# Clearing a gather buffer on GpSimd ahead of every third batch, with a batch's last gather waiting for TensorE

## The chip, the core and the metric

The kernel runs on one core of a Trainium2 chip. The metric is the device time of one execution in microseconds (us). Each core has TensorE (PE; PEld is its weight load), VectorE (DVE), ScalarE (ACT), GpSimd (POOL) and SyncE (SP), each working through its own queue in order; they meet through semaphores. Matrix products land in PSUM, everything else on the chip lies in SBUF. GpSimd issues the indirect DMAs here: gathers that fetch rows of a table in HBM by an index for each partition.

## What is computed

One layer of a graph network with 12,500 nodes of 160 channels (64 scalars and 32 vectors of 3) and 400,000 edges. The edges are sorted by destination; sources are random. Cut to what matters:

```python
h  = relu(layernorm(x))                                  # 12500 x 160
s0, s1 = h0 @ W_sc0 * a, einsum(h1, W_sc1) * a           # own part of a node
y0, y1 = h0 @ W_l1_0 * a, einsum(h1, W_l1_1) * a         # what its edges carry
w  = silu(edge_length @ fc_W1 / 4) @ fc_W2 / 8           # 400000 x 192, weights of an edge
ys0, ys1 = y0[src], y1[src]                              # the gather
mid0 = concat(w_a * ys0 * e0,  w_d * dot(ys1, e1) / sqrt(3))
mid1 = concat(w_b * ys0 x e1,  w_c * e0 * ys1)
z0, z1 = scatter_add(mid0, dst), scatter_add(mid1, dst)  # sums by destination
out = x + C_S * s + C_X * concat(z0 @ W_l2_0, z1 @ W_l2_1) * a
```

## The kernel before

The first stage makes `y` for all nodes and writes it to `y_d` in HBM. The main stage, of which the change is a part, goes through the 400,000 edges in 3125 tiles of 128 edges, an edge on each partition. Four tiles (`GT`) make a batch; there are 782 batches (`NB`), the last but one with two tiles and the last with three.

For one batch `b` the work goes through the engines like this:

- `load(b)`, L571 to L584: GpSimd issues one gather per tile (L579), 128 rows of 160 floats out of `y_d`, into a slice of the batch's buffer `yg` of 128 x 4 x 160. `yg` has eleven buffers (`YB`). For 24 of the batches, named in `made_at`, no gather is made: TensorE computes the rows from gathered rows of `x`, in pieces spread over earlier batches.
- `hidden(s)`, L592, and `activate`, L597: the inner layer of the edge weights, for two batches at a time.
- `weigh(b)`, L609 and L611: TensorE makes the edge weights in one of two PSUM banks `pw`; ScalarE puts the edge's vector beside them.
- `lift_rows(b)`, L521: ScalarE multiplies each gathered slice by a scalar of the edge, into `yge`. It is the first to read `yg`.
- `dots_of(b)`, L526 and L528, and `products(b)`, L532 to L537: VectorE forms the messages `pr` from `pw`, `yg` and `yge`. L528 writes a part of `yg`. L537 is the last reader of the batch's `pw`.
- `select(u)`, L628: VectorE makes the one-hot matrices `sel` for three batches.
- `sums(b)`, L648: TensorE adds the messages by destination. At the end of a group of 24 or 12 tiles the sum is turned (L662), mapped (L675) and added to the result (L693).

The loop over batches writes these down in an order by hand, in which a step of the loop makes the weights of batch `b + 2`, the products of `b + 1`, the sums of `b`, and loads batch `b + 10` (`AHEAD`):

```python
                if b + 2 < NB:
                    weigh(b + 2)
...
                    products(b + 1)
                if b + AHEAD < NB:
                    load(b + AHEAD)
...
                    sums(b)
```

The order holds for the engines named in `tc.manual_schedule(...)` at L796: TensorE, ScalarE and VectorE. GpSimd and SyncE are not named, so a planner places their instructions by its own costs. A gather has to wait for the old readers of its slice of `yg`. In addition the first gather of batch `b` is given a wait by hand, for the last matmul of the weights of batch `b - 8` (L582 to L584), so that gathers run no further ahead of the weights.

Of the kernel before, what the change touches and what calls it, by code (L numbers as in the profile page):

```python
# [31 lines left out]
EG = 8  # L32
YB = 11
AHEAD = 10
WIDE = 3, 5
GN = 8
HN = 2
# [9 lines left out]
def kernel(  # L47
# [19 lines left out]
    nc = tc.nc  # L67
# [5 lines left out]
    NU = (T + TG - 1) // TG  # L73
    wide = T * WIDE[0] // WIDE[1] // (EG * TG) * (EG * TG)
    starts = list(range(0, wide, 2 * TG)) + list(range(wide, T, TG))
# [36 lines left out]
    def made(b):  # L112

        return made_at.index(b) if b in made_at else None
# [173 lines left out]
    def load_xe(blk):  # L288

        if blk not in blocks:  # L290
            xe = ld.tile([P, 512], F32, name="xe")
            v = e16[blk * P:(blk + 1) * P, :].rearrange("(s k f) (h c) -> k s (f h) c", s=4, k=2, h=2)
            for k in range(2):
                nc.sync.dma_start(xe[:, 256 * k:256 * (k + 1)], v[k])
            blocks[blk] = xe

    def e4_load(q):

        if q * EG < NU and q not in raws:
            lo, hi = q * EG * TG, min((q + 1) * EG * TG, TP)  # L300
            raw = ld.tile([P, EG * TG, 4], F32, name="raw")
            nc.sync.dma_start(raw[:, :hi - lo, :].rearrange("p t c -> p (t c)"), e4[:, lo * 4:hi * 4])
            raws[q] = raw
# [26 lines left out]
    engines = {mybir.EngineType.PE, mybir.EngineType.Activation, mybir.EngineType.DVE}  # L330
# [210 lines left out]
    with (  # L541
# [9 lines left out]
        leaving, weighed = [], {}  # L551
# [13 lines left out]
        def first_of(b):  # L565
            return min(b * GT if b <= short else short * GT + (T - short * GT) // 2 if b < NB else T, T)

        def tiles_of(b):
            return list(range(first_of(b), first_of(b + 1)))

        def load(b):  # L571
            r = made(b)
            if r is not None:
                rows[b] = xms[r]
                return
            yg = ygp.tile([P, GT, D], F32, name="yg")
            rows[b] = yg
            for k, t in enumerate(tiles_of(b)):
                ins = nc.gpsimd.indirect_dma_start(  # L579
                    out=yg[:, k, :], out_offset=None, in_=y_d,  # L580
                    in_offset=bass.IndirectOffsetOnAxis(ap=src_sb[:, t:t + 1], axis=0))
                if k == 0 and b - AHEAD + 2 in weighed:  # L582
                    tc.add_manual_dep(ins.ins, weighed[b - AHEAD + 2], mybir.DependencyInfo(
                        mybir.DependencyClass.Sync, mybir.DependencyReason.DATA), reason="no further ahead of the weights")  # L584

# [37 lines left out]
        def select(u, pw):  # L623

            n = min(TG, T - u * TG)
            sels[u] = selp.tile([P, TG, WN], F32, name="sel")
            for_each = pw[:, :, SP:].unsqueeze(1).to_broadcast([P, n, GT, WN // GT])
            nc.vector.tensor_tensor(sels[u][:, 0:n, :].rearrange("p t (k c) -> p t k c", k=GT), for_each,  # L628
                                    drel[:, u * TG:u * TG + n].unsqueeze(2).unsqueeze(3).to_broadcast(
                                        [P, n, GT, WN // GT]), ALU.is_equal)  # L630

        def dots_of(b):
            tmp = part.tile([P, GT, 3, M1], F32, name="tmp")
            dot(tmp, wts[b], rows[b], len(tiles_of(b)))
# [158 lines left out]
            for f in todo:  # L793
                f()

        order = tc.manual_schedule(engines={mybir.EngineType.PE, mybir.EngineType.Activation, mybir.EngineType.DVE})  # L796
        with order:
            e4_load(0)
            for blk in range(min(AHEAD - 1, NB - 1) * GT // BT + 1):
                load_xe(blk)  # L800
            for b in range(min(AHEAD - 1, NB)):
                load(b)
# [11 lines left out]
            dots_of(0)  # L814
            if AHEAD - 1 < NB:
                load(AHEAD - 1)
            select(0, wts[0])
# [3 lines left out]
            for g, e in enumerate(last_batch):  # L821
                at_end = e + 4 >= NB
                t = e + (1 if at_end else 2)
# [5 lines left out]
            for b in range(NB + 3):  # L829
                u, k = divmod(b, K)  # L830
# [22 lines left out]
                if b + AHEAD < NB:  # L853
                    load(b + AHEAD)
# [17 lines left out]
    with (  # L872
# [11 lines left out]
        with tc.For_i(0, n, 1) as _:  # L884
# [4 lines left out]
            with tc.For_i(0, TP // GT, 1) as g:  # L889
# [14 lines left out]
                yg = fp.tile([P, GT, D], F32, name="f_yg")  # L904
# [100 lines left out]
```

## Time and profile before

| | us |
|---|---|
| median of 3 runs | 4740.17 |
| lowest and highest run | 4738.69 to 4745.56 |
| profiled execution, whole | 4710.4 |
| profiled execution, span from first to last instruction | 4708.5 |
| busy time of TensorE, VectorE, ScalarE, GpSimd | 4005.0, 3520.9, 1764.2, 2970.4 |
| the 3029 gathers at L579, busy | 2874.5 |
| mean granted clock of TensorE | 0.916 |

The profile is one execution. A row of a group names the line, the engine, the operation, what it writes and reads, how often it ran, its busy time in us and the mean of one in ns, and then the engine's idle time just before and what ended it. "issue" is idle time for which the profile shows no other reason, and "remote" is a wait whose end it cannot name. A row of a stretch of time has its bounds and length in us, the busy time of the engine and the number of its instructions, the clock granted to TensorE (1 is full), the busy share of the DMA engines and GB/s. A matmul's end in the trace is modelled.

### The profile page before, as it was taken

The numbers are of one execution on the slowest core, as the hardware profiler recorded it, in microseconds if no ns is written. First come the engines' busy times: TensorE is split into PE (matmuls) and PEld (weight loads), VectorE is DVE, ScalarE is ACT, GpSimd is POOL, SyncE is SP. The second block draws the span as 40 slices with busy tenths as digits, with TensorE's granted clock in tenths as the row PEclk, the third lists the DMA queues.
The fourth block names the chain that finished last, engine by engine and source line by source line (L and its number), as shares of the span: only waits on it lengthen the run. The fifth ranks groups of instructions, "written<-read, shape, count | busy, mean of one in ns | idle before, by whom it ended". The sixth has DMA issues, their size and how long they took to land. (4 is left out here: it accounts for less than half of the span.)

```text
span 4708.5 us, 55993 instructions
## 1 busy us (share of the span) xinstructions
PE 4005.0 (85%) x16409; PEld 2323.1 (49%) x16409; DVE 3520.9 (75%) x6817; ACT 1764.2 (37%) x5610; POOL 2970.4 (63%) x3132
## 2 busy tenths in 40 slices
PE   4578888888888888888888888988888888888888
PEld 4444554444545554444444444555455455555554
DVE  4467777777777777777777777777777777777777
ACT  4333333333333333333333333333333333333333
POOL 5566666666666666666666666666666666666663
PEclk8689999999999999999999988999999999989899
DMA  7422222222222222222222222222222222232222
GB/s 215 122 62 63 67 65 68 68 61 66 65 69 66 66 67 65 63 65 68 67 65 66 65 64 62 66 67 62 68 62 66 62 68 62 68 107 64 63 63 58
DMA packets 228622, 335.20 MB, mean 71 GB/s; under 512 B 55098, under 2 KB 171910, under 8 KB 228054
## 3 DMA queue, kind: packets, MB, share of 16 engines
q0 software_dynamic: 150000, 256.20, 22.2%
q1 hardware_dynamic: 64642, 67.02, 4.6%
q10 hardware_dynamic: 13668, 8.36, 0.6%
q8 instruction: 130, 2.13, 0.2%
q14 instruction: 182, 1.49, 0.1%
HBM read 307.49 MB, written 23.88 MB: 70 GB/s over the span
## 5 line engine op out<-in xcount | busy, mean ns | idle before, releaser
L579 POOL DMA_INDIRECT yg<-y_d,src_sb x3029 | 2874.5, 949 | 1610.9 <-issue 711.1
L648 PE MATMUL pz<-pr,sel 128*128 128x384 f32 x6250 | 2488.7, 546 | 32.0 <-issue 16.3
L648 PEld LDWEIGHTS pz<-pr,sel 128*128 128x128 f32 x6250 | 1249.1, 210 | 979.0 <-issue 429.0
L609 PE MATMUL pw<-w,hT 64*128 64x192 f32 x6250 | 810.7, 366 | 553.4 <-issue 295.7
L611 ACT ACTIVATE pw<-raw 128x12 f32<-128x12 f32 (+1 forms) x782 | 140.4, 180 | 2812.0 <-remote 1339.0
L521 ACT ACTIVATE yge<-yg,raw 128x160 f32<-128x160 f32 x3029 | 1042.0, 422 | 0.3 <-DMA yg<-y_d,src_sb 0.3
L609 PEld LDWEIGHTS pw<-w,hT 64*128 64x128 f32 x6250 | 538.6, 195 | 944.7 <-issue 545.7
L526 DVE TENSOR_TENSOR tmp<-yg,pw 128x384 f32<-128x384 f32 (+1 forms) x758 | 416.6, 550 | 561.3 <-ACT pw L611 534.9
L533 DVE TENSOR_TENSOR pr<-pr,pw 128x768 f32<-128x768 f32 (+1 forms) x782 | 745.2, 953 | 27.0
L528 DVE TENSOR_REDUCE yg<-tmp 128x128 f32<-128x384 f32 (+1 forms) x758 | 450.3, 594 | 403.0 <-ACT yge L521 348.3
L628 DVE TENSOR_TENSOR sel<-pw,drel 128x1536 f32<-128x1536 f32 (+1 forms) x261 | 455.3, 1744 | 0.0
L592 PE MATMUL px<-xe,w 32*128 32x512 f32 x782 | 439.4, 643 | 11.1 <-issue 8.6
L532 DVE TENSOR_TENSOR pr<-pw,yg 128x384 f32<-128x384 f32 (+1 forms) x758 | 420.2, 554 | 17.8
L537 DVE TENSOR_TENSOR pr<-pw,yge 128x384 f32<-128x384 f32 (+1 forms) x782 | 428.3, 548 | 0.0
L536 DVE TENSOR_TENSOR pr<-pw,yge 128x256 f32<-128x256 f32 (+1 forms) x782 | 326.4, 417 | 0.0
L597 ACT ACTIVATE hT<-px 128x512 f32<-128x512 f32 x391 | 228.7, 585 | 12.4 <-issue 11.5
L592 PEld LDWEIGHTS px<-xe,w 32*128 32x128 f32 x782 | 114.7, 184 | 209.3 <-issue 142.9
L675 PEld LDWEIGHTS px<-wc,za 128*128 128x128 f32 x1110 | 151.3, 194 | 39.6 <-issue 7.6
L693 DVE SCALAR_TENSOR_TENSOR acc<-os,by,acc 128x160 f32 x370 | 144.2, 390 | 14.4 <-ACT os L680 1.1
L675 PE MATMUL px<-wc,za 128*128 128x96 f32 x1110 | 150.0, 272 | 0.8 <-ACT za L666 0.6
L376 POOL DMA_INDIRECT xr<-in_x,src_sb x88 | 87.2, 991 | 67.7 <-issue 27.8
L662 PEld LDWEIGHTS pz<-ident,zs 128*128 128x128 f32 x555 | 72.4, 141 | 58.1 <-issue 33.9
(126 smaller groups left out, 1683.1 us busy)
## 6 DMA issues: line engine op xcount, KB each, us to landing
yg<-y_d,src_sb POOLq DMA_INDIRECT x3029
xe<-in_e SPq DMA_DIRECT2D x196, 128.0 KB
xr_d<-xr SPq DMA_DIRECT2D x24, 320.5 KB
y_d<-ys ACTq DMA_DIRECT2D x12, 640.0 KB
xm<-xr_d SPq DMA_DIRECT2D x24, 320.0 KB
acc<-in_x SPq DMA_DIRECT2D x11, 640.0 KB
out<-acc SPq DMA_DIRECT2D x11, 640.0 KB
raw<-in_e SPq DMA_DIRECT2D x32, 192.0 KB
```

The source lines that it names most:

```text
L521: nc.scalar.activation(yge[:, k, :], yg[:, k, :], AF.Copy, scale=e4v[:, k, 0:1])
L526: nc.vector.tensor_tensor(tmp[:, :n], y1, wt[:, :n, NW:NW + 3].unsqueeze(3).to_broadcast([P, n, 3, M1]), ALU.mult)
L528: nc.vector.tensor_reduce(yg[:, :n, M0:96], tmp[:, :n].rearrange("p t c u -> p t u c"), AX.X, ALU.add)
L532: nc.vector.tensor_mul(pr[:, :n, 0:96], wt[:, :n, 96:NW], yg[:, :n, 0:96])
L533: nc.vector.tensor_mul(pr[:, :n, 256:].rearrange("p t (c u) -> p t c u", c=3), pr[:, :n, 0:M0].unsqueeze(2).to_broadcast([P, n, 3, M0]), w ...
L536: nc.vector.tensor_mul(pr[:, :n, 96:160], wt[:, :n, 0:M0], yge[:, :n, 0:M0])
L537: nc.vector.tensor_mul(pr[:, :n, 160:256].rearrange("p t (c u) -> p t c u", c=3), wt[:, :n, M0:96].unsqueeze(2).to_broadcast([P, n, 3, M1] ...
L579: ins = nc.gpsimd.indirect_dma_start(out=yg[:, k, :], out_offset=None, in_=y_d, in_offset=bass.IndirectOffsetOnAxis(ap=src_sb[:, t:t + 1], ...
L592: nc.tensor.matmul(ph, w1[r, :], xe[r, :], start=True, stop=True)
L609: last = nc.tensor.matmul(pw[:, k, 0:NW], hids[s][r, o:o + P], w2[r, :], start=True, stop=True)
L628: nc.vector.tensor_tensor(sels[u][:, 0:n, :].rearrange("p t (k c) -> p t k c", k=GT), for_each, drel[:, u * TG:u * TG + n].unsqueeze(2).un ...
L648: nc.tensor.matmul(z_ps[g], sels[t // TG][:, t % TG, :], pr[:, k, M0:], start=first, stop=last)
```

## The change

Three edits. `load` counts the batches that it is called for; when it has been called at least three times (`REST`) since the last clearing, and the batch is number ten or later and is gathered, GpSimd first writes zeros to the batch's whole buffer `yg` (128 x 640) and then once more to the slice of the first gather (128 x 160). The gathers then overwrite all four slices. The wait for the weights of batch `b - 8` moves from the first gather of a batch to its last. And GpSimd (`Pool`) joins the engines that keep the order written by hand in the main stage.

```diff
+REST = 3
...
+        rested = [0]
+
         def load(b):
             r = made(b)
+            rested[0] += 1
             if r is not None:
                 rows[b] = xms[r]
                 return
             yg = ygp.tile([P, GT, D], F32, name="yg")
             rows[b] = yg
-            for k, t in enumerate(tiles_of(b)):
+            if rested[0] >= REST and b >= AHEAD:
+                nc.gpsimd.memset(yg, 0.0)
+                nc.gpsimd.memset(yg[:, 0, :], 0.0)
+                rested[0] = 0
+            of = tiles_of(b)
+            for k, t in enumerate(of):
                 ins = nc.gpsimd.indirect_dma_start(
                     out=yg[:, k, :], out_offset=None, in_=y_d,
                     in_offset=bass.IndirectOffsetOnAxis(ap=src_sb[:, t:t + 1], axis=0))
-                if k == 0 and b - AHEAD + 2 in weighed:
+                if k == len(of) - 1 and b - AHEAD + 2 in weighed:
                     tc.add_manual_dep(ins.ins, weighed[b - AHEAD + 2], mybir.DependencyInfo(
                         mybir.DependencyClass.Sync, mybir.DependencyReason.DATA), reason="no further ahead of the weights")
...
-        order = tc.manual_schedule(engines={mybir.EngineType.PE, mybir.EngineType.Activation, mybir.EngineType.DVE})
+        order = tc.manual_schedule(engines={mybir.EngineType.PE, mybir.EngineType.Activation, mybir.EngineType.DVE,
+                                            mybir.EngineType.Pool})
```

## The prediction

> **What bounds the kernel now.** I read the page first, for the shares of the engines and the chain of work that ended last.
>
> ```profile
> span 4708.5 us, 55993 instructions
> ...
> PE 4005.0 (85%) x16409; PEld 2323.1 (49%) x16409; DVE 3520.9 (75%) x6817; ACT 1764.2 (37%) x5610; POOL 2970.4 (63%) x3132
> ...
> PE 20%; issue 5%; DVE 4%; another core or an unknown queue 3%; ACT 3%; POOL 1%; DMA 0%; DVEq 0%; ACTq 0%; POOLq 0%
> ```
>
> The columns are busy time and share of the span. TensorE is busiest; GpSimd (POOL), the engine that the change touches, has 1% of the chain. Next the table of waits: who waited for whom, total, times, longest.
>
> ```profile
> ACT pw L611 <- PE pw L609: 712.1, 169, 9.3
> DVE tmp L526 <- ACT pw L611: 555.7, 236, 17.5
> DVE yg L528 <- ACT yge L521: 348.3, 276, 1.7
> PEld pw L609 <- DVE pr L537: 335.1, 201, 5.3
> PE pw L609 <- DVE pr L537: 251.9, 136, 15.4
> POOL yg L579 <- PE pw L609: 155.6, 75, 4.2
> ```
>
> The first five rows are a ring. The weights of a batch (L609) go through ScalarE (L611) to the first VectorE product (L526), and the last VectorE product (L537) frees the PSUM bank in which TensorE makes the weights after next. GpSimd is on the receiving end only: it waits for L609. Whether it is ever waited for stands in the group of the ScalarE operation that reads a gathered row, and what room it has in its own time in the stretch 300 to 4600 us, asked once for the gathers (L579) and once for an operation that runs once per batch (L611).
>
> ```profile
> L521 ACT ACTIVATE yge<-yg,raw 128x160 f32<-128x160 f32 x3029 | 1042.0, 422 | 0.3 <-DMA yg<-y_d,src_sb 0.3
> ...
> 300.00:4600.00 4300.00, 2768.78 (x2918) 0.93 0.26 66
> ...
> 300.00:4600.00 4300.00, 135.18 (x753) 0.93 0.26 66
> ```
>
> In the whole run ScalarE sat idle for 0.3 us because of a gather. 753 batches in 4300 us make 5.71 us a batch. How long a gather takes from start to start is in the timeline of GpSimd (start, duration, and in brackets the idle time before and its end):
>
> ```profile
> 541.63 0.95 POOL L579 DMA_INDIRECT yg<-y_d,src_sb  x1 [0.30 <-issue]
> 542.88 0.94 POOL L579 DMA_INDIRECT yg<-y_d,src_sb  x1 [0.30 <-issue]
> 546.79 0.94 POOL L579 DMA_INDIRECT yg<-y_d,src_sb  x1 [2.97 <-remote]
> 548.04 0.95 POOL L579 DMA_INDIRECT yg<-y_d,src_sb  x1 [0.31 <-ACT yge L521]
> 549.29 0.95 POOL L579 DMA_INDIRECT yg<-y_d,src_sb  x1 [0.30 <-issue]
> 550.55 0.95 POOL L579 DMA_INDIRECT yg<-y_d,src_sb  x1 [0.30 <-issue]
> ```
>
> It is 1.25 us (546.79 to 550.55 is three of them), of which 0.30 us is issue. So 2918 gathers fill 2918 x 1.253 = 3656 us of the 4300 and 644 us are true waiting: 644 / 753 = 0.855 us a batch, or 2.57 us in three batches. That 2.57 us is the number against which the change has to be held.
>
> **The wait, and the order of GpSimd.** The change moves the wait for TensorE from a batch's first gather to its last, and has GpSimd keep the written order. In the trace there is one wait in four gathers, but not at which of the four. The end of the program tells: by the code the last batch has three tiles and the one before it two.
>
> ```profile
> 4645.53 0.95 POOL L579 DMA_INDIRECT yg<-y_d,src_sb  x1 [0.30 <-ACT yge L521]
> 4646.78 0.95 POOL L579 DMA_INDIRECT yg<-y_d,src_sb  x1 [0.30 <-issue]
> 4648.04 0.94 POOL L579 DMA_INDIRECT yg<-y_d,src_sb  x1 [0.31 <-ACT yge L521]
> 4649.29 0.95 POOL L579 DMA_INDIRECT yg<-y_d,src_sb  x1 [0.30 <-issue]
> 4651.86 0.95 POOL L579 DMA_INDIRECT yg<-y_d,src_sb  x1 [1.62 <-DVE yg L528]
> ```
>
> Of the last three gathers it is the third that waited, 1.62 us, not the first. So the planner, left free on GpSimd, already puts the gather that bears the wait behind the others of its batch. Writing that order down changes which of a batch's four slices arrives last, and nothing else: cost 0. What is queued behind the waiting gather is only the next batch's clearing and gathers; who waits for those is ScalarE at L521, eight batches later, 8 x 5.71 = 45.7 us. If I misread this and three gathers of each batch do start a batch earlier, the cost is still 0, since nobody waits for a gather. SP's queue stays with the planner.
>
> **The clearings.** The counter starts at 0 and counts every batch, so the first clearing comes at batch 10, then in every third batch, 251 in the stretch of 753, some 258 in all. Each is two memsets, 128x640 and 128x160. The trace has three memsets of this kind, at the start, and the gather that follows them:
>
> ```profile
> 0.75 0.23 POOL L347 MEMSET acc<- 128x160 f32 x1 [0.29 <-POOLq L994]
> 0.92 0.20 POOL L255 MEMSET w<- 128x128 f32 x1
> 1.06 0.51 POOL L262 MEMSET wor<- 128x480 f32 x1
> 2.71 1.09 POOL L376 DMA_INDIRECT xr<-in_x,src_first  x1 [1.14 <-DMA src_first<-in_src]
> ```
>
> From 160 to 480 columns is 0.28 us more, so 640 columns take 0.51 + 0.14 = 0.65 us, and the part takes 0.23 us. At the least the part hides behind the whole as here (0.92 - 0.75 = 0.17 us apart) and no gap is added: 0.65 + 0.17 = 0.82 us. At the most the step from memset to gather costs the 1.14 us seen here in place of 0.30, the gather 1.09 in place of 0.95, and the step from gather to memset another 0.30: 0.65 + 0.23 + 0.84 + 0.14 + 0.30 = 2.16 us. The 1.14 us is put down to a load, so I take the issue gap of 0.30 us twice at most and less for one of them: 1.2 us. Both ends are under 2.57. So 251 x 1.2 = 301 us of GpSimd's 644 us of waiting become memset, and 343 us remain (438 at the low end, 102 at the high one). What hides the work is thus the wait for L609 itself: GpSimd comes to its waiting gather later, but over three batches still in time, and where it is late for a batch or two, the 45.7 us of lead hide that. If that cover is gone, each further microsecond in a clearing costs 251 us.
>
> A clearing must wait until the buffer's old readers are done, the products of the batch eleven before (eleven buffers). By the code those finish before the weights two batches later can be made in the same PSUM bank, and these are earlier than the ones for which the previous batch's last gather has just waited. So this wait is free, too. The readers wait for the gathers, as before.
>
> **Does a memset slow VectorE?** Against this stands that VectorE is in the ring, and a clearing might hold it up; the trace has the two side by side once, while the three memsets above ran, and one VectorE memset without company:
>
> ```profile
> 0.89 0.17 DVE L238 MEMSET wn<- 128x128 f32 x1
> 1.04 0.22 DVE L239 MEMSET wnr<- 128x192 f32 x1
> ...
> 1.27 0.27 DVE L130 MEMSET iota<- 128x256 f32 x1
> ...
> L882 DVE MEMSET f_zero<- 128x384 f32 x1 | 0.4, 378 | 0.0
> ```
>
> 0.05 us per 64 columns from 128 to 256 leads to 0.37 us at 384, and the lone one took 0.378: company cost a write nothing. It does not show operations that read two SBUF tensors, or VectorE's faster forms. Those of the main loop with the most time:
>
> ```profile
> L693 DVE SCALAR_TENSOR_TENSOR acc<-os,by,acc 128x160 f32 x370 | 144.2, 390 | 14.4 <-ACT os L680 1.1 <-issue 0.2
> L727 DVE TENSOR_SCALAR m_oh<-iota,lo_f 128x128 f32<-128x128 f32 x96 | 30.4, 316 | 0.0
> L725 DVE TENSOR_SCALAR m_h<-xm,m_mv 128x160 f32<-128x160 f32 x96 | 28.5, 297 | 0.0
> ```
>
> Together 203 us, 4.3% of the span. If each held or was held by a memset beside it, 258 x 0.88 us = 227 us of memset meet them for 227 x 0.043 = 10 us, at most all on the path. The lower end is 0. I take 0, by the memset rows, which are nearest; 10 us is the upper end.
>
> [...]
>
> **The sum.** Wait and order 0, clearings 0, VectorE 0 (to +10): the profiled execution stays at 4710.4 us, which is the span of 4708.5 and 1.9 around it. The median of the runs is 4740.2, 29.8 above it. Forecast: 4740 us. About 0.2%, 9.5 us, is what a measurement of this kernel can tell from no change.
>
> **The rivals.** (a) Slower: VectorE is held by the clearings. The place is the ring, at L526 to L537; it decides from 9.5 / 258 = 0.04 us lost per clearing. Over the 4.3% it is +10 us, 4750; if every VectorE operation is held, VectorE being busy 75% of the time, up to 227 x 0.75 = 170 us, 4910. For it: VectorE is in each of the ring's waits. Against it: the memset rows. Chance 0.24, mostly near the low price.
>
> (b) Slower: GpSimd becomes the bound, from 2.57 us a clearing on. At 3.5 us it is 251 x 0.93 = 233 us, 4973. The trace speaks against it (2.16 at most). [...] Chance 0.04.
>
> (c) Faster: the pauses pay. TensorE has stops in the weights for which the trace names nobody:
>
> ```profile
> PE pw L609 <- issue: 295.7, 277, 10.0
> ```
>
> If part of them comes from gathers that run without a break (GpSimd's stream and its packets beside TensorE's own supply), a pause each third batch spares some. A tenth is 30 us, 4710. For it: 295.7 us without a cause, in the ring. Against it: the number of gathers is the same, and DMA engines are 26% busy in the stretch. Chance 0.26.
>
> (d) The order or the clearings move TensorE's phase to a worse pattern of waits, by the same size: 4770. Chance 0.06.
>
> **How the numbers follow.** The forecast has 0.40, all of it within 0.2%. Faster is (c), 0.26. Slower is (a), (b) and (d), 0.34. The range reaches down past (c)'s 4710 to 4706, a tenth and a little of those stops, and up to 4776, past (d) and the low price of (a); about 0.2 is left out, (b), the dear half of (a), and a larger (c). Within 4732 to 4750 lies the forecast's own range.
>
> **What would show it.** Right: L521's idle time for a gather stays under a few microseconds; GpSimd's group of L579 keeps 949 ns; its waits for TensorE and unnamed ones shrink by about 300 us; two memset groups of some 258 with about 650 and 230 ns; VectorE's means at L526 to L537 and L693 unchanged; the share of POOL in the chain stays at 1%. Wrong: L521 waiting for gathers for tens of microseconds (b); longer VectorE means (a); fewer unnamed stops at L609 or a higher granted clock than 0.93 in the stretch (c), or a lower one (d).

## The result, and the profile after

The change made the kernel slower. In one comparison the kernel before took 4739.4 us and the changed one 4862.6 us (medians of four runs each): 123 us apart; the recorded ratio of the runs is 1.0255, with a 95% interval of 1.024 to 1.027. The profiled executions are 148 us apart (4710.4 and 4858.5 us; spans 4708.5 and 4856.6). The forecast was 4740 us, no change, with a range from 4706 to 4776.

The page of the changed kernel, the lines that answer to those shown of before. The gathers are now at L588, the clearings at L583 and L584, the lift at L522, the first product at L527, the weights at L618 and ScalarE's part of them at L620.

```profile
span 4856.6 us, 57024 instructions
...
PE 4050.7 (83%) x16409; PEld 2343.5 (48%) x16409; DVE 3518.6 (72%) x6817; ACT 1762.5 (36%) x5610; POOL 3188.2 (66%) x3648
...
L588 POOL DMA_INDIRECT yg<-y_d,src_sb x3029 | 2866.4, 946 | 1529.6 <-issue 727.5
...
L620 ACT ACTIVATE pw<-raw 128x12 f32<-128x12 f32 (+1 forms) x782 | 140.4, 180 | 2959.7 <-remote 1319.9
L522 ACT ACTIVATE yge<-yg,raw 128x160 f32<-128x160 f32 x3029 | 1041.9, 422 | 0.3 <-issue 0.3
...
L527 DVE TENSOR_TENSOR tmp<-yg,pw 128x384 f32<-128x384 f32 (+1 forms) x758 | 416.2, 549 | 714.5 <-issue 389.8
...
L583 POOL MEMSET yg<- 128x640 f32 x258 | 167.7, 650 | 0.1
```

Its groups by form give the second memset, its table of waits the ring, and the page of before the two rows that answer to L620 and L527:

```profile
L584 POOL MEMSET yg<- 128x160 f32 x258 | 59.6, 231 | 14.8
...
ACT pw L620 <- PE pw L618: 891.9, 193, 10.5
DVE tmp L527 <- issue: 393.2, 111, 14.9
PE pw L618 <- DVE pr L538: 359.6, 180, 14.6
POOL yg L588 <- PE pw L618: 187.0, 108, 2.8
POOL yg L588 <- POOL yg L584: 100.7, 212, 0.5
```

```profile
L611 ACT ACTIVATE pw<-raw 128x12 f32<-128x12 f32 (+1 forms) x782 | 140.4, 180 | 2812.0 <-remote 1339.0
...
L526 DVE TENSOR_TENSOR tmp<-yg,pw 128x384 f32<-128x384 f32 (+1 forms) x758 | 416.6, 550 | 561.3 <-ACT pw L611 534.9
```

The pieces have the sizes that were forecast: 258 clearings, 650 and 231 ns, a gather at 946 ns, the busy times of VectorE and ScalarE unchanged, the lift still waiting 0.3 us in the whole run. GpSimd's busy time grew by 218 us, the 227 us of memset less 8 us by which the gathers were shorter. TensorE's busy time grew by 46 us, at a granted clock of 0.906 rather than 0.916. What went wrong is that the end moved too: ScalarE's idle time before L620 went from 2812 to 2960 us, by the same 148 us as the profiled execution, and VectorE's before the first product from 561 to 715. Of the named waits, ScalarE's for the weights' matmuls went from 712 to 892 us, and TensorE's for the last VectorE product from 252 to 360. The rows count the stretch from 300 to 4600 us as before, first for the gathers, then for L620:

```profile
300.00:4600.00 4300.00, 2668.71 (x2820) 0.92 0.25 64
...
300.00:4600.00 4300.00, 130.82 (x729) 0.92 0.25 64
```

That is 729 batches rather than 753, so 17.70 us for three batches rather than 17.13. A clearing and its step take 1.11 us of GpSimd's time, as the timeline of the changed kernel shows (start, duration, idle before and its end):

```profile
2509.81 0.92 PE L618 MATMUL pw<-w,hT 64*128 64x192 f32 x8
...
2512.74 0.94 POOL L588 DMA_INDIRECT yg<-y_d,src_sb  x1 [0.30 <-issue]
...
2515.98 0.18 ACT L620 ACTIVATE pw<-raw 128x12 f32<-128x12 f32 x1 [9.54 <-PE pw L618]
...
2516.16 0.94 POOL L588 DMA_INDIRECT yg<-y_d,src_sb  x1 [2.48 <-PE pw L618]
...
2517.11 0.65 POOL L583 MEMSET yg<- 128x640 f32 x1
2517.81 0.23 POOL L584 MEMSET yg<- 128x160 f32 x1
2518.52 0.95 POOL L588 DMA_INDIRECT yg<-y_d,src_sb  x1 [0.47 <-POOL yg L584]
```

From the end of a gather at 2517.10 to the start of the next at 2518.52 are 1.42 us in place of 0.30: 1.12 us more. Over all clearings the mean is 1.11. The gathers and their gaps take 2820 x 1.246 = 3514 us of the 4300, the 243 clearings of this stretch 270, and 516 us are left as waiting: 0.71 us a batch rather than 0.855, or 2.12 us in three batches rather than 2.57. So of the 1.11 us about 0.45 came out of GpSimd's waiting and about 0.57 made the three batches longer (the rest is that the gathers came every 1.246 us rather than 1.253). 258 x 0.57 = 147 us, nearly all of the 148 between the two profiled executions.

The same timeline shows why waiting was no spare time. The weights at 2509.81 end at 2510.73, but ScalarE, which waits for them, starts at 2515.98, 5.25 us later, and GpSimd's waiting gather 0.18 us after that. In the meantime GpSimd had run its gathers without a break, up to 2513.68. Measured over 776 batches of the trace, from the fifth on (start of ScalarE's part less the modelled end of the batch's eight matmuls), that delay has a mean of 2.35 us before (median 1.74) and 2.92 us after (median 2.44). It is the signal that is late and not ScalarE: in the trace of before ScalarE waited and started more than 1 us after the matmuls' end in 344 of these batches, and in 338 of them an update of TensorE's counter is recorded 0.07 us ahead of its start. So GpSimd waits for a signal that is late, and the signal was later in the run in which GpSimd had more to do.

### The profile page after: what moved, and what is told of

It reads as the page before. It is cut to its first block, busy times and chain, and to the rows that moved or that the text cites. A ratio compares the mean times of both kernels' runs of the same rounds, so it can differ in the third digit from the quotient of the medians.

```text
span 4856.6 us, 57024 instructions
## 1 busy us (share of the span) xinstructions
PE 4050.7 (83%) x16409; PEld 2343.5 (48%) x16409; DVE 3518.6 (72%) x6817; ACT 1762.5 (36%) x5610; POOL 3188.2 (66%) x3648
## 5 line engine op out<-in xcount | busy, mean ns | idle before, releaser
L588 POOL DMA_INDIRECT yg<-y_d,src_sb x3029 | 2866.4, 946 | 1529.6 <-issue 727.5
L657 PE MATMUL pz<-pr,sel 128*128 128x384 f32 x6250 | 2523.6, 551 | 131.3 <-ACT za L675 99.0
L618 PE MATMUL pw<-w,hT 64*128 64x192 f32 x6250 | 811.7, 369 | 547.3 <-DVE pr L538 359.6
L620 ACT ACTIVATE pw<-raw 128x12 f32<-128x12 f32 (+1 forms) x782 | 140.4, 180 | 2959.7 <-remote 1319.9
L522 ACT ACTIVATE yge<-yg,raw 128x160 f32<-128x160 f32 x3029 | 1041.9, 422 | 0.3 <-issue 0.3
L618 PEld LDWEIGHTS pw<-w,hT 64*128 64x128 f32 x6250 | 542.7, 197 | 929.6 <-DVE pr L538 423.8
L527 DVE TENSOR_TENSOR tmp<-yg,pw 128x384 f32<-128x384 f32 (+1 forms) x758 | 416.2, 549 | 714.5 <-issue 389.8
L583 POOL MEMSET yg<- 128x640 f32 x258 | 167.7, 650 | 0.1
```

The costliest lines, as they stand in the source:

```text
L522: nc.scalar.activation(yge[:, k, :], yg[:, k, :], AF.Copy, scale=e4v[:, k, 0:1])
L527: nc.vector.tensor_tensor(tmp[:, :n], y1, wt[:, :n, NW:NW + 3].unsqueeze(3).to_broadcast([P, n, 3, M1]), ALU.mult)
L588: ins = nc.gpsimd.indirect_dma_start(out=yg[:, k, :], out_offset=None, in_=y_d, in_offset=bass.IndirectOffsetOnAxis(ap=src_sb[:, t:t + 1], ...
L618: last = nc.tensor.matmul(pw[:, k, 0:NW], hids[s][r, o:o + P], w2[r, :], start=True, stop=True)
L657: nc.tensor.matmul(z_ps[g], sels[t // TG][:, t % TG, :], pr[:, k, M0:], start=first, stop=last)
```

## The experiments

All of the later comparisons ran on four chips on which the kernel before takes 3966 us (medians of 3965.9 to 3966.9) rather than 4740; I take the chip of the first comparison to be another one, and call it the first chip. This must be known to read the numbers. The instructions are the same; the delay just told of is 0.16 us in `e1_order`, a run on one of these chips, rather than 2.35. So the experiments tell what the change's parts cost where the signal is punctual. All ratios are against the kernel before on the same chip; "the change" is the changed kernel.

Three theories were set against each other, and the expectations use their names. **Stretch**: a clearing costs because it makes GpSimd's unbroken run of instructions longer. In the first expectations this meant that the signal from the weights arrives only after that run has stopped; for the chips with 3966 us it came to mean that GpSimd's stream of gathers itself sets the time. **Waits**: the clearing adds a wait on GpSimd to the lift on ScalarE and to the first product on VectorE, and these cost the time. **Order**: GpSimd's written order, with the moved wait for TensorE, costs it.

**The change whole, and its order alone.** `e6_after` is the change without any edit.

> The changed kernel again, so that it stands beside the others on one chip. On a chip where the kernel before needs about 3966 us (GpSimd's gathers are its bound there): the clearings add their whole 258 x 1.12 us = 289 us, about 4255 us. On a chip where it needs about 4740 us (TensorE's signal for the weights comes late): about 4860 us.

`e1_order` is the change without the clearings:

```
-            if rested[0] >= REST and b >= AHEAD:
-                nc.gpsimd.memset(yg, 0.0)
-                nc.gpsimd.memset(yg[:, 0, :], 0.0)
-                rested[0] = 0
```

> The changed kernel without its clearings: only the written order of GpSimd and the wait at the last gather are left. Theories: (stretch) the clearings lengthen GpSimd's unbroken run of instructions, and the weights' signal from TensorE to ScalarE arrives only after that run has stopped; (waits) the cleared batches give ScalarE's first lift and VectorE's first product one more wait each, on GpSimd, and that wait slows the ring; (order) the written order alone costs it. Stretch: 4740 us, as before. Waits: 4740 us. Order: about 4860 us.

The change took 4269.3 us, 1.0764 (1.0746 to 1.0782), 303 us more, or 1.17 us for each clearing. The order alone took 3966.5, ratio 1.000 (0.999 to 1.001): moving the wait for TensorE and fixing GpSimd's order cost nothing. The page and the waits of `e1_order` show what bounds the kernel here:

```profile
PE 3686.5 (93%) x16409; PEld 2165.9 (54%) x16409; DVE 3513.2 (88%) x6817; ACT 1895.0 (48%) x5610; POOL 2980.0 (75%) x3132
...
L584 POOL DMA_INDIRECT yg<-y_d,src_sb x3029 | 2877.7, 950 | 923.4 <-issue 729.2
...
ACT yge L522 <- DMA yg<-y_d,src_sb: 755.2, 899, 4.0
```

Its gathers (L584 there) have 923.4 / 3029 = 0.305 us of idle time before each, which is the issue gap and no more: they run back to back from start to end, though GpSimd is 75% "busy" by the page. The lift, which never waited on the first chip, waits for them 899 times. With the clearings in, it waits twice as much, and GpSimd heads the chain of work that ended last (9% of it in `e1_order`), here the waits and the page of `e6_after`:

```profile
ACT yge L522 <- DMA yg<-y_d,src_sb: 1621.7, 1864, 4.3
...
POOL 27%; DVE 26%; DMA 17%; issue 16%; PE 10%; ACT 1%; SPq 1%; DVEq 1%; POOLq 0%; ACTq 0%
```

In this trace, too, a clearing and its step add 1.11 us to GpSimd's stream: 258 x 1.11 = 286 of the 303 us. Most of the rest is that the gaps before the other gathers are longer, 0.310 us rather than 0.305 on average.

**The wait for TensorE.** `e5_nowait` is the change without the written wait, `e8_free` leaves out both the wait and the clearings; the lines taken out are

```
-                if k == len(of) - 1 and b - AHEAD + 2 in weighed:
-                    tc.add_manual_dep(...)
```

> The changed kernel with its clearings, but without the hand-written wait of the gathers for TensorE; gathers then wait only for their buffers. It tells whether the late signal has to do with GpSimd waiting for the same counter of TensorE as ScalarE. If it has, the signal is on time and the kernel is faster than 4740 us. If only the length of GpSimd's work matters, it stays near 4860 us or above. Waits: about 4860 us, since the added waits are untouched.

> No clearings, and no hand-written wait of the gathers for TensorE. Where GpSimd is the bound: as before, 3966 us, within 1%. Where the signal is late: if GpSimd's waiting for the same counter makes it late, well under 4740 us, towards 4000; if not, 4740 us.

4269.5 us (1.0764, 1.0746 to 1.0782) and 3966.5 us (0.9999, 0.9989 to 1.0009): the same as with the wait, with and without clearings. A wait for which GpSimd never comes too early cost nothing here.

**The clearings without a reader.** `e2_spare` keeps GpSimd's 800 columns of memset but writes them to a buffer that nobody reads, so that no wait is added anywhere:

```
+        spare_sb = keep.tile([P, 3 * D], F32, name="spare_sb")
...
-                nc.gpsimd.memset(yg, 0.0)
-                nc.gpsimd.memset(yg[:, 0, :], 0.0)
+                nc.gpsimd.memset(spare_sb, 0.0)              # 480 columns
+                nc.gpsimd.memset(spare_sb[:, 0:2 * D], 0.0)  # 320 columns
```

> Two memsets of the same total length (480 and 320 columns) at the same places, but into a spare buffer that nobody reads, so that no engine waits for them. Stretch: about 4860 us, since GpSimd loses the same 1.1 us in each third batch. Waits: 4740 us. Order: 4860 us, the same as the run without clearings.

4243.9 us, 1.0698 (1.068 to 1.0716): 278 of the 303 us come without any added wait. The other 25 are as much as the clearing of the real buffer is longer in GpSimd's stream (1.11 us against 1.00 in the traces, x 258 = 28 us).

`e3_column` is the reverse: all the added waits, but next to no memset, `nc.gpsimd.memset(yg[:, 0, M0:M0 + 1], 0.0)` in place of the two.

> One memset of a single column of the gather buffer in place of the two: the added waits of ScalarE and VectorE are all there, GpSimd's own time grows by some 0.3 us in each third batch instead of 1.1. Stretch: a quarter of the slowdown, about 4770 us. Waits: about 4860 us. Order: 4860 us.

3990.5 us, 1.0058 (1.0041 to 1.0075), 0.095 us for each clearing, where the memset takes 118 ns. In its trace 258 instructions on ScalarE and 258 on VectorE wait for GpSimd's counter, as many as in the change, so the waits alone are worth at most that.

`e7_place` puts the spare memsets before the batch's last, waiting gather rather than before its first, `e9_double` issues them twice.

> The memsets into the spare buffer stand just before a batch's last gather, the one that waits for TensorE, and not before its first. Where GpSimd is the bound without a pause (3966 us), the place is nothing: 4245 us, as with the spare buffer before the first gather. Where GpSimd stops for TensorE's signal: if the signal follows the landing of the last gather, the memsets fit into that stop and cost nothing, 4740 us; if it follows the end of GpSimd's work, 4860 us.

> The memsets into the spare buffer twice over, so GpSimd loses about 2 x 1.08 = 2.2 us in each third batch. Stretch, where GpSimd is the bound (3966 us): 258 x 2.2 = 556 us more, about 4520 us. Where TensorE's signal is late (4740 us): more than the 120 us of the single clearing, some 4990 us if it is in proportion, and GpSimd's share of busy time as with the single one. A theory in which only the number of clearings counts: as with one.

4238.5 us (1.0686, 1.0668 to 1.0703): the place within the batch made 5 us of difference (4243.9 in `e2_spare`). 4491.1 us (1.132, 1.1287 to 1.1353): 524 us, 2.03 us a clearing, 1.9 times the 278 us of `e2_spare`, where the step in the trace is 1.98 rather than 1.00 us. No room shows up below which a clearing is free: even the 118 ns of `e3_column` cost 25 us.

`e14_half` issues one spare memset of 320 columns only.

> The change with one GpSimd clearing of 320 columns into a buffer that nobody reads (0.37 us) in place of the two. Theory (GpSimd's stream is the bound, so each clearing's own time and its step are added): 0.37 + 0.09 to 0.12 us, 258 x 0.47 = 121 us, 4075 to 4100 us where before takes 3966. Rival (a clearing has room up to some length and costs only what is over it): 3966 to 4000 us. Where before takes 4740 us: theory of a 40% share that comes through, 4780 to 4800 us; rival 4740.

4026.6 us, 1.0145 (1.0113 to 1.0177): 60 us, 0.23 a clearing, between the two expectations and in neither. The timeline of `e14_half` has the reason:

```profile
2509.82 0.95 POOL L588 DMA_INDIRECT yg<-y_d,src_sb  x1 [0.30 <-issue]
2510.77 0.38 POOL L584 MEMSET spare_sb<- 128x320 f32 x1
2511.32 0.95 POOL L588 DMA_INDIRECT yg<-y_d,src_sb  x1 [0.17 <-issue]
```

From 2510.77 to 2511.32 are 0.55 us, 0.25 more than the usual gap of 0.30. The memset begins without a gap, and the gap behind it is 0.17; why it is shorter than 0.30 is not shown. With two memsets it was not shorter: in `e2_spare` the same step is 1.31 us for 0.88 us of memset and a gap of 0.37. So the price follows what GpSimd's stream gets longer by (0.24 us on average in `e14_half`, x 258 = 62 us), not the sum of the memsets' durations.

**The clearings on another engine.** `e13_on_scalar` lets ScalarE write the zeros, to the same buffers, in the same batches. Against what was expected, not all waits stay as they were: no lift and no product waits for GpSimd any more, and the batch's first gather waits for ScalarE.

```
+        zero_sb = keep.tile([P, D], F32, name="zero_sb")
+        nc.gpsimd.memset(zero_sb, 0.0)
...
-                nc.gpsimd.memset(yg, 0.0)
-                nc.gpsimd.memset(yg[:, 0, :], 0.0)
+                nc.scalar.activation(yg, zero_sb.unsqueeze(1).to_broadcast([P, GT, D]), AF.Copy)
+                nc.scalar.activation(yg[:, 0, :], zero_sb, AF.Copy)
```

> The change with the same two clearings done by ScalarE (a copy of zeros to the whole buffer and to its part) rather than GpSimd; the gathers, the lifts and the products wait as in the change. ScalarE needs about 2.0 us for both, 258 x 2.0 = 516 us of its idle time. Theory (a clearing costs because it stands in GpSimd's stream): most of the 303 us comes back, 3966 to 4030 us where before takes 3966. Rival (the added waits, or the writing of the buffer itself, cost the time): 4200 us or more. Where before takes 4740 us: theory 4730 to 4790, rival 4860.

3966.1 us, 1.0000 (0.9989 to 1.0012). The groups by form of `e13_on_scalar` show ScalarE's clearings:

```profile
L585 ACT ACTIVATE yg<-zero_sb 128x640 f32<-128x640 f32 x258 | 186.2, 722 | 0.0
...
L586 ACT ACTIVATE yg<-zero_sb 128x160 f32<-128x160 f32 x258 | 86.8, 337 | 8.2
```

They take 1.06 us a clearing rather than the 2.0 expected. 273 us of additional ScalarE work cost nothing, 227 us of additional GpSimd work 303. With `e2_spare` (GpSimd's time without the waits: 278 us) and `e3_column` (the waits with next to none of GpSimd's time: 25 us at most) this settles it on these chips: neither the writing of the zeros nor the waits for it cost the time; the clearing's place in GpSimd's stream does.

**Taking work out of that stream.** Here gathers are replaced by loads of fixed rows on another queue, so these slices do not hold the rows of the edges:

```
+                if k == 1 and b % 3 == 1 and b >= AHEAD:
+                    nc.sync.dma_start(yg[:, k, :], y_d[0:P, :])
+                    continue
```

`e4_on_sync` does that to one gather of every third batch, without clearings; `e11_both` does it in the change with its clearings; `e12_quarter`, without clearings, does it in every batch (no `b % 3 == 1`).

> No clearings; in each third batch from the tenth on, one of the four gathers is left out and SyncE loads 128 fixed rows into its slice in its place (so these rows are not those of the edges). GpSimd has 1.25 us less in three batches, about as much as a clearing adds. Stretch: faster than before, by up to 258 x 1.25 = 322 us where GpSimd is the bound, as far as VectorE and TensorE let it, about 3700 to 3800 us; where the signal is late, by about as much as the clearings cost there, 120 us, 4620 us. Waits or order: as before.

> The change with its clearings, and one gather of every third batch (k = 1) replaced by a load of fixed rows on SyncE's queue, so that its output differs in those rows. Theory (GpSimd's own time is the bound): a clearing adds 1.17 us to GpSimd's stream and a gather less takes 1.25 us away, so the two cancel: about 3946 to 3966 us where before takes 3966. Rival (the waits that the clearings add on ScalarE and VectorE cost the time): the 303 us of the change come on top of the kernel with one gather less, 3763 + 303 = 4066 us. Where before takes 4740 us, the theory of a late signal gives 4600 to 4740, the rival over 4740.

> No clearings; one gather in every batch from AHEAD on (k = 1, a quarter of the gathers) replaced by a load of fixed rows on SyncE's queue, so that its output differs in those rows. With one in three batches replaced 204 us went. Theory (GpSimd's stream was the bound and something else took over at 3763 us): 3720 to 3765 us. Rival (GpSimd is still the bound there): three times 204 us, about 3350 us. Where before takes 4740 us: if TensorE's signal is late because of GpSimd's run of gathers, below 4400 us; if the lateness has nothing to do with GpSimd, above 4600 us.

3762.6 us (0.9487, 0.9471 to 0.9502), 3941.4 us (0.9937, 0.9914 to 0.9959) and 3748.8 us (0.9445, 0.9415 to 0.9475). In `e11_both` a clearing in and a gather out all but cancel: it lies 5 us under the range expected of Stretch and 125 under what was expected of Waits. Against the change the gather is worth 328 us, 1.27 us each, its 1.25 us from start to start. In `e4_on_sync` the same gather is worth 204 us only, because another bound comes up: `e12_quarter`, with 748 gathers gone rather than 258, gains 14 us more. Its page and waits name that bound:

```profile
PE 3623.1 (97%) x16409; PEld 2140.3 (57%) x16409; DVE 3496.3 (93%) x6817; ACT 1787.7 (48%) x5610; POOL 2270.0 (61%) x2384
...
L522 ACT ACTIVATE yge<-yg,raw 128x160 f32<-128x160 f32 x3029 | 1041.7, 420 | 7.6 <-DMA yg<-y_d,src_sb 7.5
POOL yg L587 <- PE pw L617: 599.3, 435, 5.8
```

TensorE is 97% busy, the lift no longer waits, and GpSimd now comes early to its written wait, and stands there for 599 us. The loads of fixed rows also change what the DMA queues carry, and no run separates that from the time they save GpSimd; for the clearings themselves the runs above do.

**A try at a faster version.** If gathers are dear, more batches could be computed rather than gathered: `e10_rows` is the kernel before with `RB = 23, 9` and `RS = 18, 36` (32 such batches rather than 24).

> The kernel before with more batches whose rows TensorE computes instead of GpSimd gathering them: 32 of 782 in place of 24 (RB = 23, 9; RS = 18, 36). No clearings, the old order and wait. Where GpSimd is the bound: eight batches of four gathers less, 8 x 5.0 = 40 us, less what the computed rows cost TensorE and VectorE: 3930 to 3960 us, faster than both kernels. Where TensorE's signal is late: no gain or a small loss, 4740 to 4780 us, since the ring, to which the computed rows add, is the bound.

3972.8 us, 1.0016 (1.0006 to 1.0026): no gain, where 3930 to 3960 was expected. The batches got shorter, 4.81 us on average rather than 4.87 in `e1_order`, but they began later. To compute a batch's rows, GpSimd has to gather rows of `x` for it in the first stage (L376). The groups of `e10_rows` and its timeline show it:

```profile
L579 POOL DMA_INDIRECT yg<-y_d,src_sb x2997 | 2839.2, 947 | 913.0 <-issue 671.1 <-ACT yge L521 43.6 <-DVE yg L528 37.2
L376 POOL DMA_INDIRECT xr<-in_x,src_sb x120 | 123.5, 1029 | 54.8 <-issue 25.6 <-DMA xr_d<-xr 18.6 <-ACT ys L457 3.4
...
191.30 0.95 POOL L579 DMA_INDIRECT yg<-y_d,src_sb  x1 [0.30 <-issue]
```

32 gathers fewer at L579 (2997 rather than 3029) stand against 32 more at L376 (120 rather than 88), and the first gather of `y_d` starts at 191.3 us rather than at 152.0 in `e1_order` (no trace of the kernel before was taken on these chips). The work was moved within GpSimd's stream and not taken out of it.

## Why the prediction was wrong

**The step that failed** is in the part on the clearings: "What hides the work is thus the wait for L609 itself". It treated GpSimd's 2.57 us of waiting in three batches as room, and took a clearing of 1.2 us to be free below that number. The size of the clearing was right (1.11 us, in the bounds of 0.82 to 2.16), and so was the measured waiting. The use of it was not. Waiting is room only if what is waited for comes at a time that doesn't depend on the waiting engine. On the first chip the weights' signal came later with the clearings in: GpSimd's waiting in the stretch fell by 128 us, not by the forecast's 300, and 0.57 us of every clearing came out at the end (148 us between the profiled executions, 123 between the medians). On the other chips there is no waiting at all, and a clearing costs 1.17 us, 303 us in all.

**The evidence misread** was the lift's 0.3 us of idle time. It was read as "nobody waits for a gather". It says only that the lift isn't the place where a wait shows; what got longer on the first chip is ScalarE's wait at L611 for a late signal, and VectorE's at L526 behind it. The rows that the prediction shows of the table of waits leave out two of its largest, on this very instruction:

```profile
ACT pw L611 <- remote: 1339.0, 196, 17.8
...
ACT pw L611 <- issue: 486.5, 89, 20.3
```

So more than half of ScalarE's 2812 us before L611 had no named releaser or none that fits, and where L609 is named, it had often ended microseconds before: in the 344 late batches the delay was mostly between 1.7 and 6.5 us. The prediction took the name and not the time. Nor did GpSimd's 1% of the chain speak against a cost: the shares of that chain add up to 36% of the span.

**The order and the wait: right.** Cost 0 on the later chips (`e1_order`, `e8_free`, `e5_nowait`). On the first chip no run has the order alone, but the traces of both kernels have 749 gathers that wait for TensorE's counter, and 748 of them stand at the same place in GpSimd's sequence of gathers, all but a few as the last of a batch. So the planner had indeed put them there. The row from which the prediction read this names VectorE as the releaser and doesn't show it by itself.

**Rival (a), VectorE held by the clearings: wrong as to the loss.** The measured time lies between its low and its high price, 4750 and 4910, but VectorE's busy time was 3520.9 us before and 3518.6 after. The operation with two SBUF inputs took 390 ns before and 385 after. The two tensor_scalar operations of the prediction, 297 and 316 ns before, are these in the changed kernel on the first chip, one longer and one shorter:

```profile
L734 DVE TENSOR_SCALAR m_h<-xm,m_mv 128x160 f32<-128x160 f32 x96 | 31.3, 326 | 0.0
L736 DVE TENSOR_SCALAR m_oh<-iota,lo_f 128x128 f32<-128x128 f32 x96 | 27.0, 281 | 0.0
```

On the later chips, without clearings (`e1_order`) and with them (`e6_after`), they are these, from the groups by form:

```profile
L730 DVE TENSOR_SCALAR m_h<-xm,m_mv 128x160 f32<-128x160 f32 x96 | 28.9, 301 | 0.0
L732 DVE TENSOR_SCALAR m_oh<-iota,lo_f 128x128 f32<-128x128 f32 x96 | 27.6, 288 | 0.0
```

```profile
L734 DVE TENSOR_SCALAR m_h<-xm,m_mv 128x160 f32<-128x160 f32 x96 | 32.7, 340 | 0.0
L736 DVE TENSOR_SCALAR m_oh<-iota,lo_f 128x128 f32<-128x128 f32 x96 | 30.2, 315 | 0.0
```

There they got 39 and 27 ns longer, 6.4 us together, while the one with two inputs took 388 and 387. With the memsets doubled (`e9_double`) they took 376 and 401 ns, and the one with two inputs 386. So in these runs the two tensor_scalar operations got longer with more memsets and the one with two inputs did not; why is not shown. The 6.4 us lie within the 10 us that the prediction set as the upper end. Single runs without clearings differ by as much as the smaller of these changes (m_oh took 316 ns in the kernel before on the first chip and 288 in `e1_order`), and on the first chip only m_h got longer. It isn't the loss: 6.4 us are a fiftieth of the 303, and `e2_spare`, `e3_column` and `e13_on_scalar` put the loss into GpSimd's stream.

**Rival (b), GpSimd becomes the bound: the right mechanism at the wrong price.** It was to decide only from 2.57 us a clearing on, at a chance of 0.04. `e14_half` and `e3_column` show that on the later chips it decides from the first tenth of a microsecond (25 us for 258 memsets of 118 ns in `e3_column`). A clearing with its steps took 1.11 us on average, in the changed kernel on the first chip as in `e6_after`, under the 2.16 that the prediction allowed at most and far under the 3.5 at which it priced this rival.

**Rival (c), the pauses pay: wrong.** The granted clock fell (0.916 to 0.906 over the span) and the kernel got slower. **(d)** forecast a loss, but from another phase of TensorE, and of 30 us. Its sign came, a clock of 0.92 rather than 0.93 in the stretch; whether the lower clock is a cause of the loss on the first chip or goes with it is not shown. TensorE's busy time grew by 46 us, which is the most that its longer work could account for of the 148. On the later chips the clock fell as well with the clearings (0.978 in `e1_order`, 0.956 in `e6_after`), while GpSimd's stream hardly paused there (in `e6_after` 0.310 us on average before a gather that follows no clearing).

**What stays open.** Why the weights' signal comes late on the first chip, and why less than the full 303 us came through there. In the trace of before, 176 of the 344 late signals come 1.9 to 2.6 us after GpSimd's last gather has ended; a moment taken at random from 300 us on falls there in 3% of cases. This points to GpSimd's gathers or their transfers delaying the signal, but GpSimd stops because it waits for a signal from the same engine, and no experiment ran on that chip, so this is argued and not shown, and the split between stretch and waits is shown for the other chips alone. Taking it over to the first chip rests on the result's agreeing in sign.

## What to carry to other kernels

Count idle time of an engine as room only when what ends it is independent of that engine: compare the releaser's end with the start of what it released, and where microseconds lie between, don't count the idle time as cover. For an engine that issues one gather after another, add up starts, not busy time: 75% busy with a gap of 0.305 us before each gather was full (`e1_order`). When work is taken off the engine that sets the time, count what it does elsewhere in its place: in `e10_rows` 32 gathers went and 32 others came. Small extra work belongs on the engine that is shown to have slack: the same clearings, 273 us of work, cost nothing on ScalarE (`e13_on_scalar`, 3966.1 us).

## What the runs showed of the hardware

The same program took 4740 us in the first comparison and 3966 on the four later chips, 20% apart; a chip's trace is a statement on that chip. On the slower one TensorE's granted clock was lower (0.916 against 0.978 over the span), and the ScalarE instruction that waits for the weights' matmuls came 2.35 us after them on average, against 0.16 in `e1_order`. How the 774 us divide between the two was not settled.

A gather of 128 rows of 640 bytes costs GpSimd 1.25 us from start to start, 0.95 of it shown as busy (`e1_order`). A memset placed between two gathers begins right behind the first (0.1 us of idle time before all 258 together in `e14_half` and in the changed kernel). Behind it, in the timelines from 2500 to 2520 us, the gap to the second gather was 0.17 us after one memset of 0.38 us (`e14_half`) and 0.27 after one of 0.12 us (`e3_column`), rather than 0.30; after two memsets it was 0.37 us (`e2_spare`), and 0.47 where the gather writes the cleared buffer (the changed kernel).
